# Two-layer graph attention and a typed graph convolution on one core: reordering the preparation and the list writes

## The chip, the core and the metric

The kernel runs on one core of a Trainium2 chip. Five engines work side by side, each through its own instruction queue in a fixed order: TensorE (PE, with its weight loads as PEld), VectorE (DVE), ScalarE (ACT), GpSimd (POOL) and SyncE (SP). SP, ACT and POOL also issue DMAs; the indexed ones (gathers and scatters by a column of row numbers) are all issued by POOL. The metric is the device time of one launch in microseconds.

## What is computed

There are N = 1250 nodes of D = 768 numbers and E = 20000 edges, sorted by destination, each with one of 34 types. Cut to what matters:

```python
h = relu(layernorm(x))
# layer 0: two GATv2 attentions, 8 heads and then 1 head
def gatv2(x, src, dst, Ws, bs, Wd, bd, attn):
    fs, fd = x @ Ws + bs, x @ Wd + bd
    logits = einsum('ehd,hd->eh', leaky_relu(fs[src] + fd[dst], 0.2), attn)
    alpha = softmax of logits over the edges of one dst
    return elu(segment_sum(alpha * fs[src], dst))
h1 = layernorm(gatv2(h, ..., attn1) + h) * ln1_w + ln1_b
x = x + layernorm(gatv2(h1, ..., attno)) * lno_w + lno_b
# layer 1: per (type, dst) the mean of h[src], times W_rel[type]; then a normalised graph sum
h = relu(layernorm(x))
h1 = einsum('rni,rio->no', mean_by_type, W_rel) + h @ W_root + b_rgcn
x = x + normalised neighbour sum of (h1 @ W_gcn) + b_gcn
```

Everything is float32.

## The kernel before

**Nodes and slots.** Nodes are sorted by falling in-degree ("rank order") and cut into NT = 10 tiles of 128. Tile k has `CAPS[k]` slots (33, 22, 20, 18, 17, 16, 15, 14, 13, 11, together 179): slot s of a tile holds the s-th incoming edge of each of its 128 nodes, padded. A slot is one gather of 128 source rows.

**Front** (`fast_front`). It loads the edges and x, normalises x into `hT` (columns) and `h0_d` (rows in DRAM), and finds where each node's edges begin: `got` gathers rows of `dst`, `first` counts. A product with `shift` (L832) gives the next node's start and so the degree. Keys made of degree and node number are spread over all partitions by TensorE (L859, L860), and ten VectorE comparisons (L865) count each node's rank. `rank_d` takes a row of four integers per node (node, first, degree, 0), scattered by rank (L880) and read back in rank order into `rk` (L901). With `first` in rank order, windows of 64 packed edges (type x 2048 + source) are gathered from `win_d` (L912), and five rounds of select-by-bit shift each window to its node's first edge; the result is `f.ell`, from which the source indices `f.srci` come (L931).

The source table `fs_d` (x @ W1s with a column of logit parts per head) is made tile by tile by `sources(j)`: 12 products and two bias products on TensorE, two copies on ScalarE, one write by SP. Tiles 0 and 1 are put ahead of the keys in TensorE's order, tile 2 right behind them, the others follow.

**Pairs** (`pairs`, called at the start of the first attention). For every (type, node) the edges of that type are counted and given a column and lane in a list of pairs. VectorE does nearly all of it; TensorE counts over nodes with 0/1 masks (`mask`, three rounds, L970 to L979), and its results are needed in the second half. The outcome is `place`, the list position of each edge. It goes to DRAM (`place_d`) and comes back. Then the pair list `pair_d` is filled with defaults and the tails of `h2_d` and `h1_d` with zeros (L1354 to L1373).

**Attentions** (`attention`). Per slot: one gather into a ring of 24 buffers `fs` (POOL, L1148), the maximum against the negated destination part (VectorE, L1208), the product with the attention vector and its sum (L1213 and L1214 for 8 heads, L1210 for one). Slots are taken in chunks of up to 20; after a chunk comes its softmax, and then `back`: the rows are scaled and summed on TensorE (L1268, L1258), which frees the ring buffer. While a chunk is in `back`, the next is in front. The destination part of a tile needs its rows gathered, transposed and multiplied by W1d (`negated1`, L1416). After a tile's last chunk `finish1` or `finish2` normalises and makes the next stage's inputs, with several GpSimd DMAs and, in `finish2`, two GpSimd additions.

**List writes.** `list_edges(row, slots)` follows a slot's gather. It adds `slots` to a running count and issues one scatter of an edge slot into `pair_d` (POOL, L1152) for every whole one, 179 in all. `rate` is what each slot adds, `rest` what the last slot adds. Before: 0.9 and 60 in the first attention, 0 and 0 in the second:

```python
            if s >= CHUNK or t.k:
                list_edges(row, rate)
            if t.k == NT - 1 and s == t.S - 1:
                list_edges(row, rest)
```

**After that** come the typed products (`first_half`, `second_half`: gather from `h2_d`, transpose, multiply by W_rel, add into `h1_d`), which read the list through `lists`, and the neighbour sums.

A scheduler in the tile framework sets each engine's order from the program's order and its own estimate of times; `tc.issue_after` puts one instruction behind another.

Of the kernel before, what the change touches and what calls it, by code (L numbers as in the profile page):

```python
# [10 lines left out]
F32 = mybir.dt.float32  # L11
# [7 lines left out]
P = 128  # L19
# [8 lines left out]
PT = 4  # L28
DT = 4
# [597 lines left out]
def fast_front(ctx, tc, f, x, src, dst, edge_type, W1s, b1s, W1d, b1d, attn1, attno, W_rel):  # L627
# [34 lines left out]
    rank_d = dram.tile([NP, 4], I32, name="f_rank_d")  # L662
# [9 lines left out]
    f.ell = keepp.tile([P, NT, S0], I32, name="f_ell")  # L672
# [4 lines left out]
    f.place_d = dram.tile([P, NT * S0], I32, name="f_place_d")  # L677
    f.w1d = const.tile([P, KC, D], F32, name="f_w1d")

    with ExitStack() as front:  # L680
# [110 lines left out]

        quarter = SLOPE / (1.0 - SLOPE)
# [14 lines left out]
        def sources(j):  # L807

            n = min(P, N - j * P)
            ps = ps_m.tile([P, 2, 512], F32, name="ps", tag="ag")  # L810
            for half in range(2):
                for k in range(KC):
                    nc.tensor.matmul(ps[:n, half, :QW], hT[:, k, j * P:j * P + n], w1s[:, k, half], start=(k == 0), stop=False)
                last = nc.tensor.matmul(ps[:n, half, :QW], ones_row[:, :n], bias1[:, half], start=False, stop=True)
            o = work.tile([P, H, HD + 1], F32, name="o_s", tag="o_s", bufs=3)
            ov = o.rearrange("p (a h) d -> p a h d", a=2)
            nc.scalar.copy(ov[:n, :, :, :HD], ps[:n, :, :HW].rearrange("p a (h d) -> p a h d", d=HD))
            nc.scalar.copy(ov[:n, :, :, HD], ps[:n, :, HW:QW])
            nc.sync.dma_start(f.fs_d[j * P:j * P + n, :], o[:n].rearrange("p h e -> p (h e)"))
            return last  # L820

        last = sources(0)
# [8 lines left out]
        with tc.issue_after(last.ins):  # L831
            last = nc.tensor.matmul(sh_ps[:, 0:1], shift, first[:, 0:1], start=True, stop=True)  # L832
        with tc.issue_after(last.ins):
            last = sources(1)
# [3 lines left out]


# [14 lines left out]
        with tc.issue_after(last.ins):  # L854
            for g in range(2):
                wide = ps_m.tile([P, 2, 512], F32, name="wide", tag="ag").rearrange("p a b -> p (a b)")
                for lo, hi in ((0, 512), (512, N // 2)):
                    at = slice(g * (N // 2) + lo, g * (N // 2) + hi)
                    nc.tensor.matmul(wide[:, lo:hi], ones16[:EP], flat2[:, at], start=True, stop=False)  # L859
                    last = nc.tensor.matmul(wide[:, lo:hi], big16[:EP], flat[:, at], start=False, stop=True)  # L860
                nc.scalar.copy(keys[:, g * (N // 2):(g + 1) * (N // 2)], wide[:, :N // 2])
# [7 lines left out]
        rec = prep.tile([P, NT, 4], I32, name="rec")  # L869
        nc.vector.memset(rec, 0)  # L870
        nc.vector.tensor_copy(rec[:, :, 0], node)
        nc.vector.tensor_copy(rec[:, :, 1], first[:, :NT])
        nc.vector.tensor_copy(rec[:, :, 2], deg)

        past = prep.tile([NP - N, 4], I32, name="past")
# [10 lines left out]
        with tc.issue_after(last_keys.ins):  # L886
            sources(2)


        packed = prep.tile([EP, EC], I32, name="packed")  # L890
        nc.vector.scalar_tensor_tensor(packed, ev[:, 2, :], 2048.0, ev[:, 0, :], op0=ALU.mult, op1=ALU.add)
        zrow = prep.tile([1, RW], I32, name="zrow")
        nc.vector.memset(zrow, 0)
        pk = packed.rearrange("p (r c) -> p r c", c=RW)
        nc.scalar.dma_start(win_d[1:NR + 1, :RW].rearrange("(p r) c -> p r c", p=EP), pk)
        nc.scalar.dma_start(win_d[0:NR, RW:].rearrange("(p r) c -> p r c", p=EP), pk)
        nc.scalar.dma_start(win_d[NR:NR + 1, RW:], zrow)


        rk = prep.tile([P, NT, 4], I32, name="rk")  # L900
# [3 lines left out]
        nc.vector.tensor_copy(f.degf, rk[:, :, 2])  # L904
        arow = prep.tile([P, NT], I32, name="arow")
        nc.vector.tensor_scalar(arow, rk[:, :, 1], 5, None, op0=ALU.arith_shift_right)
        nc.vector.tensor_scalar(arow, arow, float(NR - 1), 1.0, op0=ALU.min, op1=ALU.add)
        offs = prep.tile([P, NT], I32, name="offs")
        nc.vector.tensor_scalar(offs, rk[:, :, 1], RW - 1, None, op0=ALU.bitwise_and)
        win = prep.tile([P, NT, WIN], I32, name="win")  # L910
        for k in range(NT):
            nc.gpsimd.indirect_dma_start(  # L912
                out=win[:, k, :], out_offset=None, in_=win_d[:, :],
                in_offset=bass.IndirectOffsetOnAxis(ap=arow[:, k:k + 1], axis=0))
        wf = prep.tile([P, NT, WIN], F32, name="wf")
        nc.vector.tensor_copy(wf, win)
        bits = prep.tile([P, 5, NT], F32, name="bits")
        for i in range(5):
            bi = prep.tile([P, NT], I32, name="bi", tag="bi", bufs=2)
            nc.vector.tensor_scalar(bi, offs, i, 1, op0=ALU.arith_shift_right, op1=ALU.bitwise_and)  # L920
            nc.vector.tensor_copy(bits[:, i, :], bi)
        for i in (4, 3, 2, 1, 0):
            b = 1 << i
            L = S0 + b - 1
            df = prep.tile([P, NT, S0 + 15], F32, name="df", tag="df")
            nc.vector.tensor_sub(df[:, :, :L], wf[:, :, b:b + L], wf[:, :, :L])
            nc.vector.tensor_tensor(df[:, :, :L], df[:, :, :L],
                                    bits[:, i, :, None].to_broadcast([P, NT, L]), op=ALU.mult)
            nc.vector.tensor_add(wf[:, :, :L], wf[:, :, :L], df[:, :, :L])
        nc.vector.tensor_copy(f.ell, wf[:, :, :S0])  # L930
        nc.vector.tensor_scalar(f.srci, f.ell, 2047, None, op0=ALU.bitwise_and)  # L931
# [5 lines left out]
        def pairs():  # L937
# [13 lines left out]
            typ = pp.tile([P, NT, S0], I32, name="typ")  # L951
            nc.vector.tensor_scalar(typ, f.ell, 11, None, op0=ALU.arith_shift_right)
            tv = pp.tile([P, NT, S0], F16, name="tv")
            nc.vector.scalar_tensor_tensor(tv, pad, 100.0, typ, op0=ALU.mult, op1=ALU.add)
# [11 lines left out]
            for i in range(3):  # L966
# [11 lines left out]
                for k in range(NT):  # L978
                    nc.tensor.matmul(tp[:, :R], ones_b, mask[:, i, k, :], start=(k == 0), stop=(k == NT - 1))  # L979
# [3 lines left out]
                tot.append(b)  # L983

# [71 lines left out]
            pl_i = pp.tile([P, NT, S0], I32, name="pl_i")  # L1056
# [11 lines left out]
            nc.vector.scalar_tensor_tensor(pl_i, pad, float(P * COLS), pl, op0=ALU.mult, op1=ALU.add)  # L1068
            nc.sync.dma_start(f.place_d[:, :], pl_i.rearrange("p k s -> p (k s)"))

        for j in range(3, NT):
            sources(j)
        rows_only.close()
# [52 lines left out]
def fast_rest(ctx, tc, f, x, src, dst, edge_type, W1s, b1s, W1d, b1d, attn1, ln1_w, ln1_b,  # L1126
# [9 lines left out]
    h2_d = dram.tile([NP + P, D], F32, name="r_h2_d")  # L1136
    ZERO = NP + (PT + 1) * P
    h1_d = dram.tile([ZERO + 1, D], F32, name="r_h1_d")
# [33 lines left out]
    def attention(H, table, negated, attn_e, first, loads, finish, rate, rest):  # L1172
# [21 lines left out]
        def front(c, i):  # L1194
# [5 lines left out]
            if s >= CHUNK or t.k:  # L1200
                list_edges(row, rate)
# [526 lines left out]
```

## Time and profile before

| | us |
|---|---|
| time, median of 3 runs | 2796.56 (2795.64 to 2802.76) |
| the profiled execution, its own time | 2795.48 |
| its span, first to last instruction | 2793.7 |
| mean granted TensorE clock | 0.925 |

| stage | from, to (us) | DVE busy | POOL busy | PE busy |
|---|---|---|---|---|
| front, to the ranks' columns | 45 to 128 | 34.07 | 22.04 | 80.07 |
| pairs and first slots | 128 to 221 | 83.12 | 28.42 | 47.12 |
| first attention, steady | 258 to 813 | 487.90 | 432.28 | 434.67 |
| passage to the second | 813 to 908 | 62.73 | 51.92 | 79.01 |
| second attention, first half | 908 to 1131 | 208.66 | 154.66 | 141.87 |
| second attention, second half | 1131 to 1331 | 194.75 | 145.15 | 176.94 |
| typed products | 1407 to 2590 | 293.73 | 553.99 | 1172.29 |
| sums | 2590 to 2793 | 93.06 | 117.46 | 143.38 |

All rows are of one profiled execution; busy time is in us of the stretch. A line of the timeline gives start and duration in us, the engine, the line of the kernel, the operation, out<-in with sizes, the count, and in brackets how long the engine had been idle and what ended that. A line of the waits gives the total, the number of times and the longest, in us. A stall costs time only where nothing later absorbs it.

### The profile page before, as it was taken

The numbers are of one execution on the slowest core, as the hardware profiler recorded it, in microseconds if no ns is written. First come the engines' busy times: TensorE is split into PE (matmuls) and PEld (weight loads), VectorE is DVE, ScalarE is ACT, GpSimd is POOL, SyncE is SP. The second block draws the span as 40 slices with busy tenths as digits, with TensorE's granted clock in tenths as the row PEclk, the third lists the DMA queues.
The fourth block names the chain that finished last, engine by engine and source line by source line (L and its number), as shares of the span: only waits on it lengthen the run. The fifth ranks groups of instructions, "written<-read, shape, count | busy, mean of one in ns | idle before, by whom it ended". The sixth has DMA issues, their size and how long they took to land. (4 is left out here: it accounts for less than half of the span.)

```text
span 2793.7 us, 23960 instructions
## 1 busy us (share of the span) xinstructions
PE 2345.4 (84%) x7635; PEld 1354.2 (48%) x7635; DVE 1556.5 (56%) x2363; ACT 851.2 (30%) x2295; POOL 1546.9 (55%) x1131
## 2 busy tenths in 40 slices
PE   5953693788988377898789999999999999999667
PEld 3521252444444244454456666666666666665234
DVE  6589969898985899999453222222222222200263
ACT  3003774776772122333311211221221122121000
POOL 1343877777774766776275444444444544431574
PEclk9976896999999789999889999999999999999888
DMA  6144443454531766765387777777777777765785
GB/s 214 45 159 164 131 129 94 120 142 129 143 102 35 267 208 193 220 208 182 123 264 191 190 191 190 186 195 198 197 188 185 194 192 182 182 158 147 235 275 182
DMA packets 137988, 483.91 MB, mean 173 GB/s; under 512 B 26474, under 2 KB 28803, under 8 KB 137854
## 3 DMA queue, kind: packets, MB, share of 16 engines
q0 software_dynamic: 85152, 341.52, 47.1%
q1 hardware_dynamic: 48043, 134.21, 13.6%
q10 hardware_dynamic: 4658, 6.57, 0.7%
q8 instruction: 63, 1.03, 0.1%
q14 instruction: 72, 0.58, 0.1%
HBM read 392.99 MB, written 89.33 MB: 173 GB/s over the span
## 5 line engine op out<-in xcount | busy, mean ns | idle before, releaser
L1116 PE MATMUL ps<-wrel,mT 128*128 128x384 f32 x3336 | 1099.6, 486 | 1.3 <-DMA wrel<-in_L_gnn_W_rel_dram 1.3
L1116 PEld LDWEIGHTS ps<-wrel,mT 128*128 128x128 f32 x3336 | 623.4, 190 | 407.5 <-issue 1.6
L1148 POOL DMA_INDIRECT g<-r_h_d,lists x241 | 340.8, 1414 | 527.6 <-DVE g L1580 282.8
L1268 PE MATMUL ag<-fs,identf 128*128 128x384 f32 x716 | 291.1, 541 | 178.0 <-ACT fs L1266 167.8
L1580 DVE TENSOR_TENSOR g<-g,g 128x768 f32<-128x768 f32 x68 | 64.6, 950 | 620.4 <-DMA g<-r_h_d,lists 304.0
L1208 DVE TENSOR_TENSOR z<-fs,nfd 128x776 f32<-128x776 f32 (+1 forms) x358 | 347.4, 988 | 45.3 <-DMA fs<-f_fs_d,rec 24.9
L1266 ACT ACTIVATE fs<-fs,lg 128x96 f32<-128x96 f32 x1376 | 371.1, 362 | 4.6 <-issue 4.1
L1258 PE MATMUL ag<-fs,dg 128*128 128x384 f32 x716 | 252.4, 514 | 80.6 <-ACT dg L1256 80.0
L1148 POOL DMA_INDIRECT fs<-f_fs_d,rec x179 | 245.0, 1369 | 104.6 <-issue 48.1
L1152 POOL DMA_INDIRECT r_pair_d<-rec,place x179 | 245.8, 1373 | 95.0 <-issue 47.9
L1268 PEld LDWEIGHTS ag<-fs,identf 128*128 128x128 f32 x716 | 136.4, 205 | 321.1 <-ACT fs L1266 244.4
L1603 POOL DMA_INDIRECT r_h_d<-y,lists x139 | 221.8, 1596 | 109.3 <-ACT y L1602 52.9
L1148 POOL DMA_INDIRECT fs<-r_fs_d,rec x179 | 234.9, 1312 | 83.2 <-issue 33.1
L1258 PEld LDWEIGHTS ag<-fs,dg 128*128 128x128 f32 x716 | 142.1, 201 | 187.6 <-ACT dg L1256 85.7
L1602 ACT ACTIVATE y<-ps,lists 128x768 f32<-128x768 f32 x71 | 64.1, 902 | 479.8 <-PE ps L1116 473.0
L1602 ACT ACTIVATE y<-ps,rcnt 128x768 f32<-128x768 f32 x68 | 61.4, 902 | 456.3 <-PE ps L1116 456.3
L1659 DVE TENSOR_TENSOR acc<-acc,nb 128x768 f32<-128x768 f32 x86 | 82.4, 958 | 198.1 <-DMA nb<-r_h_d,srcz 194.2
L1210 DVE SCALAR_TENSOR_TENSOR z<-z,attn_o 128x769 f32<-128x769 f32 x179 | 178.4, 1015 | 0.0
L1213 DVE TENSOR_TENSOR z<-z,attn 128x776 f32<-128x776 f32 x179 | 168.8, 958 | 0.1
L1214 DVE TENSOR_REDUCE lg<-z 128x8 f32<-128x776 f32 x179 | 168.4, 953 | 0.1
L1513 DVE SCALAR_TENSOR_TENSOR arow<-node,from_f,arow 128x1250 f16<-128x1250 f16 x93 | 140.3, 1508 | 1.0
L1104 PEld LDWEIGHTS pt<-identf,g 128*128 128x128 f32 x834 | 100.5, 142 | 55.2 <-issue 24.1
(284 smaller groups left out, 2301.8 us busy)
## 6 DMA issues: line engine op xcount, KB each, us to landing
wrel<-in_L_gnn_W_rel_dram SPq DMA_DIRECT2D x37, 2304.0 KB
g<-r_h_d,lists POOLq DMA_INDIRECT x241
r_nfd_d<-fd SPq DMA_DIRECT2D x10, 384.0 KB
nfd<-r_nfd_d SPq DMA_DIRECT2D x10, 384.0 KB
r_x_d<-xb SPq DMA_DIRECT2D x10, 384.0 KB
x1r<-r_x_d SPq DMA_DIRECT2D x10, 384.0 KB
f_fs_d<-o_s SPq DMA_DIRECT2D x9, 388.0 KB
x<-in_x_dram SPq DMA_DIRECT2D x9, 384.0 KB
```

Source lines behind the costliest of these rows:

```text
L1116: last = nc.tensor.matmul(ps[:n, half, :f.HW], hT[:, k, j * P:j * P + n], w[:, k, cols], start=(k == 0), stop=(k == f.KC - 1 and not bias))
L1148: return nc.gpsimd.indirect_dma_start(out=to, out_offset=None, in_=table, in_offset=bass.IndirectOffsetOnAxis(ap=idx, axis=0))
L1152: s = nc.gpsimd.indirect_dma_start(out=table, out_offset=bass.IndirectOffsetOnAxis(ap=idx, axis=0), in_=rows, in_offset=None, **kw)
L1208: nc.vector.tensor_tensor(z, fs, t.nfd, op=ALU.max)
L1210: nc.vector.scalar_tensor_tensor(z[:, 0, :], z[:, 0, :], 1.0, attn_e[:, 0, :], op0=ALU.mult, op1=ALU.mult, accum_out=t.lg[:, s, :])
L1213: nc.vector.tensor_mul(z, z, attn_e)
L1214: nc.vector.tensor_reduce(t.lg[:, s, :], z, axis=AX.X, op=ALU.add)
L1258: nc.tensor.matmul(c.ps[:, half, :HW], dg, fs[:, 0, half * HW:(half + 1) * HW], start=begin, stop=end)
L1266: nc.scalar.activation(fs[:, h, :HD], fs[:, h, :HD], AF.Copy, scale=t.lg[:, s, h:h + 1])
L1268: nc.tensor.matmul(c.ps[:, half, :HW].rearrange("p (h d) -> p h d", d=HD), f.identf, fs[:, half * H // 2:(half + 1) * H // 2, :HD], start= ...
L1513: nc.vector.scalar_tensor_tensor(a, node16, from_f[:, k, s:s + 1], a, op0=ALU.is_equal, op1=ALU.add)
L1603: s = nc.gpsimd.indirect_dma_start(out=h1_d[:, :], out_offset=bass.IndirectOffsetOnAxis(ap=j.node, axis=0), in_=y, in_offset=None, compute ...
```

## The change

Five things are moved or resized; the arithmetic is the same.

1. `sources(0)` and `sources(1)` no longer stand ahead of the keys; `sources(0)` now follows them, and the others come after the pairs are declared.
2. Windows of edges are gathered by node number, from `first` directly, and shifted to the first edge there. The rows scattered by rank grow from 4 to 2 + 33 integers (node, degree, the packed edges). The second gather after the read-back is gone; `f.srci` and the new `f.typ` come straight from `rk`.
3. The TensorE products of `sources(7)` to `sources(9)` (`TL = 7`) are put behind the pairs' last mask product.
4. The fills of `pair_d`, `h2_d` and `h1_d` move into the front, and `place` stays in SBUF.
5. List writes start with sixteen after slot 23 of the first tile of either attention; rates become 0.7 with 0 at the end, and 0.5 with 60 at the end in the second attention.

```diff
+TL = 7
...
-    rank_d = dram.tile([NP, 4], I32, name="f_rank_d")
+    rank_d = dram.tile([NP, 2 + S0], I32, name="f_rank_d")
...
-    f.place_d = dram.tile([P, NT * S0], I32, name="f_place_d")
+    f.place = keepp.tile([P, NT, S0], I32, name="place")
...
+        fill = prep.tile([P, COLS, 3], I32, name="fill")
+        nc.vector.memset(fill[:, :, 2], 0)
...
+        nc.sync.dma_start(f.pair_d.rearrange("(p c) f -> p c f", p=P), fill)
+        zero = prep.tile([P, D], F32, name="zero")
+        nc.vector.memset(zero, 0.0)
+        nc.sync.dma_start(f.h2_d[NP:, :], zero)
+        for t in range(PT + 1):
+            nc.sync.dma_start(f.h1_d[NP + t * P:NP + (t + 1) * P, :], zero)
...
         def sources(j):
...
+            mine = []
...
-            return last
-
-        last = sources(0)
+            return mine
...
-        with tc.issue_after(last.ins):
-            last = nc.tensor.matmul(sh_ps[:, 0:1], shift, first[:, 0:1], start=True, stop=True)
-        with tc.issue_after(last.ins):
-            last = sources(1)
+        nc.tensor.matmul(sh_ps[:, 0:1], shift, first[:, 0:1], start=True, stop=True)
...
+        nc.vector.tensor_copy(begin, first[:, :NT])
+        nc.vector.tensor_scalar(arow, begin, 5, None, op0=ALU.arith_shift_right)
...
+        for j in range(NT):
+            nc.gpsimd.indirect_dma_start(
+                out=win[:EP, j, :], out_offset=None, in_=win_d[:, :],
+                in_offset=bass.IndirectOffsetOnAxis(ap=arow[:EP, j:j + 1], axis=0))
...
+        rec = prep.tile([P, NT, 2 + S0], I32, name="rec")
         nc.vector.tensor_copy(rec[:, :, 0], node)
-        nc.vector.tensor_copy(rec[:, :, 1], first[:, :NT])
-        nc.vector.tensor_copy(rec[:, :, 2], deg)
+        nc.vector.tensor_copy(rec[:, :, 1], deg)
+        nc.vector.tensor_copy(rec[:EP, :, 2:], wf[:EP, :, :S0])
...
         with tc.issue_after(last_keys.ins):
-            sources(2)
+            sources(0)
...
+        nc.vector.tensor_scalar(f.srci, rk[:, :, 2:], 2047, None, op0=ALU.bitwise_and)
+        nc.vector.tensor_scalar(f.typ, rk[:, :, 2:], 11, None, op0=ALU.arith_shift_right)
...
                 for k in range(NT):
-                    nc.tensor.matmul(tp[:, :R], ones_b, mask[:, i, k, :], start=(k == 0), stop=(k == NT - 1))
+                    ahead = nc.tensor.matmul(tp[:, :R], ones_b, mask[:, i, k, :], start=(k == 0), stop=(k == NT - 1))
...
+            for i in behind:
+                tc.add_manual_dep(i.ins, ahead.ins.name, mybir.DependencyInfo(
+                    mybir.DependencyClass.NoSync, mybir.DependencyReason.DATA), reason="the table's last tiles later")
...
-            nc.vector.scalar_tensor_tensor(pl_i, pad, float(P * COLS), pl, op0=ALU.mult, op1=ALU.add)
-            nc.sync.dma_start(f.place_d[:, :], pl_i.rearrange("p k s -> p (k s)"))
-
-        for j in range(3, NT):
+            nc.vector.scalar_tensor_tensor(f.place, pad, float(P * COLS), pl, op0=ALU.mult, op1=ALU.add)
+
+        for j in range(1, TL):
             sources(j)
+        behind = []
+        for j in range(TL, NT):
+            behind += sources(j)
...
-            if s >= CHUNK or t.k:
+            if t.k == 0 and s == ring - 1:
+                list_edges(row, 16)
+            elif t.k or s >= ring:
                 list_edges(row, rate)
...
-        attention(H, f.fs_d, negated1, f.attn_1, prepare_lists, loads1, finish1, 0.9, 60)
+        attention(H, f.fs_d, negated1, f.attn_1, prepare_lists, loads1, finish1, 0.7, 0)
...
-        attention(1, fs2_d, negated2, f.attn_o, lambda: None, loads2, finish2, 0, 0)
+        attention(1, fs2_d, negated2, f.attn_o, lambda: None, loads2, finish2, 0.5, 60)
```

## The prediction

> **What bounds the kernel now.** I read the windows by stage first, then who waited for whom inside them, then the timelines where one wait ends another. The kernel is a chain of stages with little overlap between them: front (0 to 221 us), first attention (to about 908), second attention (to about 1390), the typed products, the sums. What a stage saves or loses is passed on whole: the products that follow keep TensorE busy for 1172.29 of 1183 us and are not touched.
>
> The front, VectorE's waits between 45 and 128 us (total, times, longest):
>
> ```profile
> DVE f_perm L902 <- DMA rk<-f_rank_d: 18.8, 1, 18.8
> DVE wf L916 <- issue: 11.9, 1, 11.9
> DVE junk L865 <- ACT keys L861: 10.0, 1, 10.0
> DVE first L835 <- PE sh_ps L832: 5.4, 1, 5.4
> DVE gotf L824 <- DMA got<-in_dst_dram,row_i: 1.9, 1, 1.9
> ```
>
> 48 of 83 us are waits: for TensorE behind two tiles of the source table (L835, L865), for the ranks to go through memory and back (L902), for the edge windows gathered in rank order after that (L916). TensorE meanwhile works on the table to the end, and the pairs' products come behind it:
>
> ```profile
> 66.11 0.39 PE L859 MATMUL wide<-diag,ones 125*128 125x512 f16 x1
> ...
> 141.95 4.15 PE L813 MATMUL ps<-w1s,hT 128*98 128x388 f32 x12
> 146.03 0.89 PE L814 MATMUL ps<-bias,ones_row 1*98 1x388 f32 x2
> 146.85 0.32 PE L970 MATMUL pp<-mask,tri 128*128 128x340 bf16 x1
> ```
>
> Both attentions, busy us per engine (PE, PEld, DVE, ACT, POOL, each with its count):
>
> ```profile
> 258.00:813.00 555.00, 434.67 (x1251) 228.90 (x1249) 487.90 (x671) 382.23 (x1329) 432.28 (x307) 0.90 0.46 127
> 908.00:1131.00 223.00, 141.87 (x404) 79.89 (x403) 208.66 (x398) 51.08 (x113) 154.66 (x115) 0.82 0.70 220
> ```
>
> VectorE leads in both (88% and 94%), but a GpSimd DMA row is followed by 0.30 us of issue, so GpSimd's queue is occupied for 432.28 + 307 x 0.3 = 524 of 555 us, and for about 189 of 223. How near the second attention is to the limit is in its GpSimd timeline:
>
> ```profile
> 944.70 1.45 POOL L1148 DMA_INDIRECT fs<-r_fs_d,rec  x1 [0.30 <-issue]
> 946.45 1.53 POOL L1148 DMA_INDIRECT xt<-in_x_dram,f_permg  x1 [0.30 <-DVE lg L1223]
> 951.69 1.81 POOL L1467 TENSOR_TENSOR xt<-xt,lnb 128x768 f32<-128x768 f32 x1 [3.71 <-DMA xt<-in_x_dram,f_permg]
> 953.64 1.51 POOL L1148 DMA_INDIRECT fs<-r_fs_d,rec  x1
> ...
> 962.44 1.45 POOL L1148 DMA_INDIRECT fs<-r_fs_d,rec  x1 [0.30 <-DVE z L1208]
> 964.19 1.44 POOL L1148 DMA_INDIRECT fs<-r_fs_d,rec  x1 [0.30 <-DVE z L1210]
> 965.94 1.45 POOL L1148 DMA_INDIRECT fs<-r_fs_d,rec  x1 [0.30 <-DVE z L1208]
> ```
>
> From 955 to 980 the gathers start exactly 1.75 us apart. That is VectorE's time for a slot there (L1208 and L1210, 0.875 us from start to start each): GpSimd gets one DMA through per slot. With VectorE idle (front, 104 to 116 us) the same kind of row takes 0.95, so 1.25 with its issue. There is nearly no room for a second one per slot.
>
> **The change, part by part.** All sums are made against the profiled execution: 2795.48 us, span 2793.7. The median of the three runs, 2796.56, is 1.1 above it.
>
> (1) Sources(0) and (1) leave TensorE's queue ahead of the keys. `first` stands at 50.9; the shift product (0.4 us) now meets an idle TensorE, so L835 waits 0.6 instead of 5.4. Then 2.1 us of degrees and diagonals, to 53.7, and the keys' products with their copies, 2.45 us (66.11 to 68.56 in the trace), to 56.2: wait 2.6 instead of 10.0. Saved 12.2 us. Ranking, 10 x 1.56, ends at 72.
>
> (2) Windows in node order. Four small DVE operations of 0.1 us, ten gathers on GpSimd (0.95 + 0.30 in the trace; 1.5 + 0.3 allowed beside ranking) from 52.5 to 65 or 71, landing 2.9 us later by the attention's shortest gather-to-use time. Either is about covered by ranking: the wait of 11.9 goes. If the cover fails, 2 us come back. The 9.4 us of selection (118.15 to 127.55) stay, ahead of the scatter now, which starts at 82.5 instead of 84.7. Rows grow from 16 to 140 bytes, no more of them; ten scatters at 1.18 + 0.30 and 3.85 us to the landed read-back as now, plus at most 3 for longer rows: ranks and edges are in at 101.6. Behind the scatter on GpSimd nothing stands until the first attention; behind the read-back on SP stand the table's writes, as today (100.66 in the trace), and three `o_s` buffers carry those until about 105. The pairs start at 103.3 instead of 128.3: 25.0 saved.
>
> (3) The table. Sources(0) starts after the keys, at 55.5; a tile takes 9.91 us (57 to 147 in the trace), so seven end at 124.9. The pairs' masks, 18 us after the pairs' start as now, are there at 121.3. The products take 6.8 (146.85 to 153.6), to 131.7; the last three tiles end at 161.4, 14.6 later than now. On VectorE the part that needs no products (16 us) lasts until 137.5, so the products are hidden; the remaining pair work (26 us of the old 162 to 190 stretch and 14.6 us of picks now woven between slots) ends near 179. The rows gathered at 162, transposed and multiplied by W1d (10.4 us) are ready at 180. So VectorE waits 1 to 2 us. If the scheduler leaves picks behind that wait, up to 15 are lost: upper end.
>
> (4) The fill. 2.6 us of DVE (223.5 to 226) and eight SP writes of 2.7 MB move ahead of ranking, into time when SP has issued its loads (idle from 18.4 to 27.3) and DVE waits (4 us before 23.3); h0's writes, not read before 150, go behind them. Saved 2.6; the gather of `got` may land 1 us later. `place` stays in SBUF; its trip through DRAM was hidden.
>
> Front: -25.0 - 2.6 + 1.5 + 1 = **-25**, between -30 and -5.
>
> (5) List writes in the first attention. Sixteen go after gather 23, in the gap before the ring of 24 buffers frees (187 to 258 in the trace, four writes in it): free. Then 0.7 per slot for 155 slots: 124 in all, 55 are left. The 36 of the old remainder lie behind the last gather beside work of TensorE and VectorE (the row write they hold up is ready at 842.7, issued at 873.9, but the next user of its buffer waits for TensorE until 878.5): no gain. In the steady part about 30 writes less stand against 24.9 us, in 20 waits, in which VectorE stood for gathered rows. After such a wait it often meets the next one, for TensorE or ScalarE, so I take a third: **-9**, between -2 and -25.
>
> (6) List writes in the second attention: none before, now 16 after gather 23 and 39 over the next 78 slots. Behind gather 23 are the gathers of slot 24 on; the first of them is used 6.1 us after its issue ends (961.2), 3 of which are landing. Of the sixteen, nine go at 1.75 until VectorE runs dry at 961, seven at 1.25: 24 us later for gather 24, 3 of slack: 21 lost. Then 39 x 1.5 (between both prices) = 58 more on GpSimd. Its queue stood free between 950 and 1131 for 26 us, less the 0.3s (ring 7.5, L1089 9.2, root 5.0, den 4.2): 32 lost. Sum **+53**. Low end: 1.25 each, all gaps used, the other DMAs 0.2 faster: +18. High end: 1.75 each, nothing used: +93. I stay by the rows nearest to it. After slot 101 all is as before; VectorE can't make up for it.
>
> Here a rule speaks against the price. The Trainium skill, "SBUF — State Buffer", section "Who interferes with whom", reports a probe in which tensor_tensor and tensor_reduce did not stall DMAs that GpSimd issues, as they leave free the write interface that descriptors need. By it a write beside L1208 and L1210 costs 1.25 and the sum is -25 - 9 + 18, about -16. The rows above (1.45 at a full VectorE, 0.95 at an idle one) contradict it for these indexed DMAs, and decide.
>
> Sum: -25 - 9 + 53 = **+19**: 2814.5, and 2815 on the median's scale.
>
> **Rivals.** *The writes fit (faster).* GpSimd speeds up as VectorE pauses, the gaps take the rest, part 6 costs 10 instead of 53, part 5 gives 15: -25 - 15 + 10 = -30, 2767. For it: 34 of 223 us of the queue are free. Against: 16 writes in a row behind gather 23, and 1.75 per gather right after. It decides below a cost of about 34 for part 6. *Even.* Part 6 at 35: within a few us of now, about 2797. *The front also fails (slower).* ScalarE's dinv, which today waits 14.9 us for the degrees inside the table's copies, or SP's read of the ranks, falls one tile earlier in the order; TensorE stalls 7 us, picks stay behind the late nfd: the front saves 5 only, +39, 2835. *Not as said.* If the three tiles still ran ahead of the products, VectorE would wait from 137 to 162: front 0, 2841.
>
> **How the numbers follow.** Forecast 0.50 (2800 to 2840 alone), front fails 0.16, even 0.14, fit 0.20. About 0.3% (8 us) is what this kernel's measurement tells from no change. Faster 0.20, same 0.14, slower 0.66. Range 2780 to 2850: it leaves out the deep end of "fit" and the high end of part 6.
>
> **What would show it.** Right: keys' wait under 3 us, `win` landed before selection, pairs from 103, table end near 161, place near 180, the second attention's first z about 34 us earlier (near 879); then z waits for fs rows of 50 us instead of 19, and a second attention some 50 longer. Wrong: those waits below 30, or first z later than 895.

## The result, and the profile after

The changed kernel takes 2863.86 us (median of 4 runs) against 2799.37 for the kernel before (median of 4): ratio 1.023, 95% interval 1.0205 to 1.0255. It is 64 us slower. The forecast was 2815, with a range of 2780 to 2850. The sign was right; the time lies outside the range.

The two profiled executions (2863.54 and 2795.48 us) are read against each other at marks that both have. "First max" is the first L1236 (L1208 before) of an attention, "18th" and "21st" are that operation of the 18th and the 21st slot of the first attention; the slots end with the last such operation of an attention.

| mark (us) | before | after | difference |
|---|---|---|---|
| ranks and edges read, pairs start | 128.3 | 113.3 | -15.0 |
| table's last product | 146.1 | 180.2 | +34.1 |
| `place` made | 220.6 | 183.0 | -37.6 |
| first max | 191.7 | 206.7 | +15.0 |
| 18th slot | 251.7 | 251.9 | +0.2 |
| 21st slot | 258.4 | 273.8 | +15.4 |
| end of the first attention's slots | 844.5 | 847.0 | +2.5 |
| second attention, first max | 912.6 | 916.0 | +3.4 |
| second attention, end of its slots | 1329.9 | 1393.2 | +63.3 |
| last typed product | 2581.4 | 2642.3 | +60.9 |
| last instruction | 2793.7 | 2861.8 | +68.1 |

The column reads as four steps. The front gives nothing by the 18th slot (forecast: 25 gained). The first attention loses 15 between its 18th and 21st slot and regains 13. The second attention loses 60 (forecast: 53). The last stage, behind the typed products, takes 7 more. The second attention's first z, for which the prediction named "later than 895" as a sign of being wrong, came at 916.0.

Every mark is of one execution. In another one of the unchanged kernel after (`e14_after_again` below) the first attention's slots end at 838.6 instead of 847.0, so differences of a few us between single marks mean little.

VectorE's waits between 45 and 128 us, kernel after (total, times, longest):

```profile
DVE f_perm L954 <- DMA rk<-f_rank_d: 19.3, 1, 19.3
DVE wf L918 <- issue: 6.7, 1, 6.7
DVE gotf L853 <- DMA got<-in_dst_dram,row_i: 3.8, 1, 3.8
DVE junk L913 <- ACT keys L909: 2.2, 1, 2.2
```

The waits for TensorE ahead of the keys went as forecast. A wait for the edge windows is still there, 6.7 of the old 11.9. VectorE's timeline says why: the cast of the windows (L918) stands after the fourth of ten comparisons (L913), and the other six stand behind it.

```profile
66.60 1.51 DVE L913 TENSOR_SCALAR_CACHE_REDUCE junk<-keys,key 128x1250 bf16<-128x1250 f32 x1
68.04 0.08 DVE L913 DVE_READ_ACCUMULATOR junk<-keys,key 128x1 f32 x1
74.80 0.49 DVE L918 CAST wf<-win 125x640 f32<-125x640 int32 x1 [6.68 <-issue]
75.21 1.51 DVE L913 TENSOR_SCALAR_CACHE_REDUCE junk<-keys,key 128x1250 bf16<-128x1250 f32 x1
```

TensorE and ScalarE, kernel after: ScalarE's square root (L1382) waits 29 us for the degrees with the table's copies behind it, so TensorE stands for 11.2 us in the middle of the table.

```profile
101.01 0.91 PE L843 MATMUL ps<-bias,ones_row 1*128 1x388 f32 x2
113.15 5.17 PE L841 MATMUL ps<-w1s,hT 128*128 128x388 f32 x8 [11.23 <-ACT o_s L848]
...
180.13 0.89 PE L843 MATMUL ps<-bias,ones_row 1*98 1x388 f32 x2
```

```profile
112.04 0.30 ACT L1382 ACTIVATE dinv<-f_degf,f_ones_col 128x10 f32<-128x10 f32 x1 [29.01 <-DVE f_degf L956]
```

Behind the table's end comes the chain that VectorE now stands for, 20.5 us, with the picks long done (timeline of all engines, kernel after): gather, transposes, product, `nfd`.

```profile
185.74 0.99 POOL L1174 DMA_INDIRECT h<-f_h_d,f_permg  x1 [78.46 <-DVE nfd L1215]
194.15 1.51 PE L1133 MATMUL pt<-identf,h 128*128 128x128 f32 x6 [13.02 <-DMA bias_s<-in_L_gnn_bos_dram]
195.63 10.02 PE L1145 MATMUL ps<-f_w1d,hT 128*128 128x384 f32 x24
205.69 0.96 DVE L1421 SCALAR_TENSOR_TENSOR nfd<-ps,bias 128x768 f32<-128x768 f32 x1 [20.47 <-PE ps L1145]
```

The burst in the first attention, kernel after (timelines of POOL, ACT and DVE): the next tile's rows are gathered behind the sixteen writes, ScalarE copies their transposes ahead of the first softmax's exponent, and VectorE waits 14.3 us for that exponent.

```profile
261.05 0.97 POOL L1178 DMA_INDIRECT r_pair_d<-rec,place  x1 [0.31 <-issue]
262.33 1.00 POOL L1174 DMA_INDIRECT h<-f_h_d,f_permg  x1 [0.30 <-issue]
...
267.27 1.06 ACT L1135 COPY hT<-pt 128x384 f32<-128x384 f32 x2 [71.10 <-PE pt L1133]
269.65 0.31 ACT L1260 ACTIVATE lg<-lg 128x128 f32<-128x128 f32 x1
269.99 0.38 DVE L1262 TENSOR_REDUCE den<-lg 128x8 f32<-128x128 f32 x1 [14.33 <-ACT lg L1260]
```

The burst in the second attention, kernel after, GpSimd's timeline and then VectorE's:

```profile
962.20 1.45 POOL L1178 DMA_INDIRECT r_pair_d<-rec,place  x1 [0.30 <-issue]
963.95 0.97 POOL L1178 DMA_INDIRECT r_pair_d<-rec,place  x1 [0.30 <-issue]
...
972.89 0.97 POOL L1178 DMA_INDIRECT r_pair_d<-rec,place  x1 [0.30 <-issue]
974.17 0.99 POOL L1174 DMA_INDIRECT xt<-in_x_dram,f_permg  x1 [0.31 <-issue]
978.11 1.80 POOL L1472 TENSOR_TENSOR xt<-xt,lnb 128x768 f32<-128x768 f32 x1 [2.95 <-DMA xt<-in_x_dram,f_permg]
980.06 0.99 POOL L1174 DMA_INDIRECT fs<-r_fs_d,rec  x1
```

```profile
984.09 0.96 DVE L1236 TENSOR_TENSOR z<-fs,nfd 128x769 f32<-128x769 f32 x1 [21.29 <-DMA fs<-r_fs_d,rec]
```

VectorE runs dry at 963, and stands 21.3 us. All its waits for gathered rows in the second attention (19.1 us in 8 before):

```profile
DVE z L1236 <- DMA fs<-r_fs_d,rec: 78.8, 38, 21.3
```

### The profile page after: what moved, and what is told of

It reads as the page before. It is cut to its first block, busy times and chain, and to the rows that moved or that the text cites. A ratio compares the mean times of both kernels' runs of the same rounds, so it can differ in the third digit from the quotient of the medians.

```text
span 2861.8 us, 23950 instructions
## 1 busy us (share of the span) xinstructions
PE 2347.5 (82%) x7635; PEld 1360.0 (48%) x7635; DVE 1553.2 (54%) x2362; ACT 849.6 (30%) x2295; POOL 1555.7 (54%) x1131
## 5 line engine op out<-in xcount | busy, mean ns | idle before, releaser
L1236 DVE TENSOR_TENSOR z<-fs,nfd 128x776 f32<-128x776 f32 (+1 forms) x358 | 340.5, 964 | 99.9 <-DMA fs<-r_fs_d,rec 78.8
L1296 PE MATMUL ag<-fs,identf 128*128 128x384 f32 x716 | 284.6, 532 | 106.4 <-ACT fs L1294 95.1
L1174 POOL DMA_INDIRECT fs<-f_fs_d,rec x179 | 239.1, 1336 | 124.1 <-issue 55.0
L1178 POOL DMA_INDIRECT r_pair_d<-rec,place x179 | 264.9, 1480 | 56.4 <-issue 45.7
L1607 ACT ACTIVATE y<-ps,rcnt 128x768 f32<-128x768 f32 x68 | 61.4, 902 | 456.8 <-PE ps L1145 456.8
L1174 POOL DMA_INDIRECT nb<-r_h_d,srcz x86 | 102.0, 1186 | 47.9 <-DMA nb<-r_h_d,srcz 27.5
```

The lines of the kernel that those rows point to most:

```text
L1174: return nc.gpsimd.indirect_dma_start(out=to, out_offset=None, in_=table, in_offset=bass.IndirectOffsetOnAxis(ap=idx, axis=0))
L1178: s = nc.gpsimd.indirect_dma_start(out=table, out_offset=bass.IndirectOffsetOnAxis(ap=idx, axis=0), in_=rows, in_offset=None, **kw)
L1236: nc.vector.tensor_tensor(z, fs, t.nfd, op=ALU.max)
L1296: nc.tensor.matmul(c.ps[:, half, :HW].rearrange("p (h d) -> p h d", d=HD), f.identf, fs[:, half * H // 2:(half + 1) * H // 2, :HD], start= ...
```

## The experiments

They ran on several chips, on which the kernel before took 2777 to 2795 us (medians); times are therefore given as ratios to the kernel before on the same chip, with their 95% intervals, and marks and waits are of one profiled execution each. On one of these chips the kernel after stood at 1.0238 (1.0203 to 1.0273).

**The lists apart from the front.** `e1_lists_before` is the kernel after with the old condition and rates:

```diff
-            if t.k == 0 and s == ring - 1:
-                list_edges(row, 16)
-            elif t.k or s >= ring:
+            if s >= CHUNK or t.k:
                 list_edges(row, rate)
...
-        attention(H, f.fs_d, negated1, ..., 0.7, 0)
+        attention(H, f.fs_d, negated1, ..., 0.9, 60)
...
-        attention(1, fs2_d, negated2, ..., 0.5, 60)
+        attention(1, fs2_d, negated2, ..., 0, 0)
```

> The changed front with the list writes as in the kernel before (0.9 a slot over the first attention from slot 16 on, the rest at its end, none over the second, no burst of sixteen). Theory L (the loss is the 55 list writes over the second attention): the second attention goes from 477 us (first max to last, kernel after) back to 417, the first attention, which gets 51 writes more, grows from 640 to about 652; time 2864 - 60 + 12 = about 2816. Rival A (a list write costs the same wherever it stands, the front is what lost): the two attentions together stay within 10 us of the kernel after, time 2854 or more.

`e2_lists_only` is the reverse: the kernel before with only these lines changed.

> The kernel before with only the changed rates of list writes (16 behind the 24th gather of each attention, 0.7 a slot, then 0.5 a slot in the second). Theory L: second attention 477 instead of 417 with one wait of about 21 us at the burst, first attention about 10 shorter at most; time 2799 + 60 - 10 = about 2849; what is left between that and the 2864 of the kernel after, 15 us, is then the changed front's. Rival A: within 10 us of 2799, the front bears the whole of the loss.

e1: 1.0017 (0.9997 to 1.0037), second attention 415.5 us. e2: 1.0153 (1.0127 to 1.0179), second attention 477.1. The waits of VectorE there, e1 and then e2:

```profile
DVE z L1234 <- DMA fs<-r_fs_d,rec: 19.2, 11, 8.2
```

```profile
DVE z L1210 <- DMA fs<-r_fs_d,rec: 79.5, 42, 21.3
```

The second attention's 60 us belong to the list writes, whatever the front. Rival A fell, and e1 says that the new front alone gives nothing measurable. e1's first attention did not grow to 652 as I wrote, but took 632.7; it lacks the burst's 15 us. (In the code the single writes of before start at slot 20, `CHUNK`, and not at 16 as this and later expectations say.)

The two ratios add up to 1.017, not 1.024, some 20 us less. Two things are in the marks. In the old front the burst does not disturb the first attention (18th to 21st slot 6.7 us; 21.9 in the kernel after). And in e2 the old front itself was faster than in the profile of before: its 18th slot came at 242.3 instead of 251.7, with VectorE's operations in the same order. Between 160 and 193 us VectorE pauses for 8.4 us in before (8.8 in e8 below, which has the old front too), none of them put down to another engine or a DMA, and for 0.4 in e2, a wait for TensorE. The same operation, before and then e2:

```profile
175.86 0.51 DVE L1011 TENSOR_TENSOR pdf<-pdf,xcol 128x340 f32<-128x340 f32 x1 [1.79 <-issue]
```

```profile
169.97 0.51 DVE L1011 TENSOR_TENSOR pdf<-pdf,xcol 128x340 f32<-128x340 f32 x1
```

No kernel with the new front has such pauses there. What makes them was not tried. So how much a front gains depends on the execution it is held against: by e2's 18th slot the new front loses 9.6 us instead of 0.2.

**Bursts.** `e9_no_second_burst` and `e12_no_first_burst` take one burst each out of the kernel after (`if H > 1 and t.k == 0 ...`, `if H == 1 and t.k == 0 ...`).

> The kernel after without the burst of sixteen in the second attention: all of its 55 writes come at 0.5 a slot. If the burst's wait (21.3 us) is a cost of its own, the second attention falls from 477 to about 456 and the time by 0.7%. If GpSimd is the bound there and each write costs its own time wherever it stands, the wait of 21.3 us goes and the same time comes back as more and smaller waits for gathers: second attention 470 or more, time within 7 us of the kernel after.

> The kernel after without the burst of sixteen in the first attention; the second attention gets its burst and, with 16 more writes left over, 0.5 a slot for longer. If the burst costs the first attention what the slots show (from the 18th to the 21st slot 21.9 us instead of 7.5): the 21st slot's max at about 259 instead of 273.8 and the first attention's end 12 to 15 us earlier, then 16 writes more over the second attention at about 1.1 us each, 17 us: the time within 6 us of the kernel after. If the first attention is bound by VectorE over its length and the burst's stall is taken up: its end within 4 us of 847, and the time 15 us longer than the kernel after's.

e9: 1.0221 (1.0187 to 1.0255), second attention 469.5 instead of 477.2 (in an execution 15 us faster than e9's median). The wait of 21.3 is gone and most of its time is back as small waits:

```profile
DVE z L1236 <- DMA fs<-r_fs_d,rec: 69.9, 48, 9.4
```

So most of what a write costs there is its own time on GpSimd, wherever it stands; the burst adds 8 us at most, and the two kernels' ratios do not tell them apart. That it is GpSimd's queue and not the traffic of the DMAs fits the second attention's windows: with 0.30 us for each of its operations GpSimd is occupied for about 448 of 477 us in the kernel after (362 of 418 before), while the DMA engines' busy share falls from 0.69 to 0.62. e12: 1.0245 (1.0226 to 1.0263); 18th to 21st slot 7.5 us as expected, and the 16 writes more make the second attention 491.7. What the first attention gains between those slots (14.4) the second loses (14.5): the total stays where it was.

`e16_first_burst_only` puts the first burst into the mended kernel described below, with all writes over the first attention.

> The mended front with all list writes over the first attention (0.9 a slot, the rest at its end), and with the burst of sixteen behind its 24th gather in place of the single writes of slots 16 to 23: as many writes as in the mended kernel, only bunched. If the burst costs what the slots of the kernel after show: the 21st slot's max 15 us later than in the mended kernel, and of that 10 us or more still there at the first attention's end; time about 12 us longer. If the first attention takes the stall up later: the same 15 at the 21st slot, less than 4 at the end, same time.

18th to 21st slot 24.7 us instead of 7.5, time 1.0011 (0.9985 to 1.0037) against the mended kernel's 0.9986 on the same chip: medians 2795.35 and 2783.50, 12 us. In the two profiled executions the first attentions end within 1 us of each other; but the mended one's execution was itself 8.7 us above its median, so I go by the medians, and where the 12 us are carried stays unshown. Nor is it the bunching alone: with single writes from slot 20 on, the sixteen replace about four writes, so that twelve more fall into the first attention and twelve fewer behind its last gather.

**Writes in the passage.** `e8_before_slow_lists` is the kernel before with 0.7 a slot from slot 24 and the rest at the first attention's end.

> The kernel before with its list writes at 0.7 a slot from slot 24 on instead of 0.9 from slot 16 on, no burst, and all that are left (about 70) at the end of the first attention, none over the second. Theory L': the 24 us that the first attention's end gained with the changed rates in the front of before came from fewer writes beside it, and the second attention's loss is apart from it: first attention's end at about 822, of the 70 writes (about 100 us of GpSimd at 1.45) some 20 to 40 us stick out past the passage between the attentions, so the second attention's first max is near 905 and the time within 10 us of before. Rival: the burst or the order that goes with it made that gain: first attention's end at 840 or later, time 2815 or more.

1.0071 (1.0047 to 1.0095): slower by more than expected. The first attention's slots end at 824.5 instead of 844.5, so theory L' was right that fewer writes there save time (20 us for 34 writes, 0.6 each); but 54 writes in the passage push the last row of `fs2_d` from 61.4 to 99.1 us behind that (37.7 for 34 more, 1.1 each). The second attention's price in the kernel after is 60 / 55 = 1.1 each. Of the three places the first attention is the cheapest in these executions, and that is where most of them had been.

**The front's waits.** `e3_dinv_late` and `e5_win_after` take away one wait each:

```diff
+        with tc.issue_after(f.last_table):
             nc.scalar.activation(f.dinv, f.degf, AF.Sqrt, ...)
...
+        with tc.issue_after(ranked.ins):
             nc.vector.tensor_copy(wf[:EP], win[:EP])
```

> The kernel after with one instruction of ScalarE, the square root of the degrees, put behind the table's last copy; the read of the ranks stays on the SyncE queue between the table's writes. Theory F (that instruction holds ScalarE and so TensorE): the stall of 11.2 us at 101.9 goes or shrinks to under 3, since ScalarE still has one free buffer of three when the writes stand behind the read; the table ends near 170 instead of 181, the first max falls at about 196 instead of 207, and if the front's end sets the first attention's the time is about 2854. Rival S (the read on SyncE is as bad as the instruction): stall 8 or more, table end 178 to 181, time 2861 to 2864. Rival R (the first attention takes up a late start): first max 10 earlier, its end unmoved, time 2862.

> The kernel after with the cast of the gathered windows put behind the last comparison of the ranking (in the kernel after it stands behind four of ten and waits 6.7 us for the windows). Theory F: the wait goes, the rank scatter starts at 86 instead of 92.7, the pairs at 106.6 instead of 113.3, TensorE's stall behind ScalarE falls from 11.2 to about 4.5, the table ends at 174, first max at about 200, time 2857. Rival R: the same marks earlier but the first attention's end unmoved, time 2863.

`e6_front_fix` has both, and the read of the ranks on GpSimd's queue (`nc.gpsimd.dma_start(rk, ...)`); `e7_front_fix_lists_before`, "the mended kernel", has the old list writes as well.

> The kernel after with three orders changed in the front: ScalarE's square root behind the table, the windows' cast behind the ranking, and the read of the ranks on the GpSimd queue, which has nothing else there, so that no write of the table stands behind it. The list writes are as in the kernel after. Theory F (what the front lost is these waits): no stall of TensorE in the table, table from 60 to about 160 with the products between, pairs from 106, first max at about 183 to 186 instead of 207, first attention's end about 22 earlier than in the kernel after, time about 2.0% less than the kernel after's less what the burst takes, ratio to before about 1.015. Rival P (one of the two waits hides the other, so each of them alone gives what both give): first max at 190 or later, ratio 1.019.

> The same three orders and the list writes as in the kernel before. If the front's gain, forecast at 25 us, is there once its waits are gone: first max 183, first attention about 633 long as in the run with the list writes of before, its end about 816, time about 25 us under that run, ratio to before about 0.993. If the first attention takes up an earlier start (bound by the gathers or the picks): its end within 8 us of 841, ratio 1.000 or more.

| | after | e3 | e5 | e6 | e7 |
|---|---|---|---|---|---|
| table's last product | 180.2 | 165.5 | 168.8 | 165.5 | 167.0 |
| first max | 206.7 | 195.2 | 190.7 | 190.4 | 188.9 |
| 18th slot | 251.9 | 240.4 | 235.8 | 235.6 | 234.1 |
| 21st slot | 273.8 | 257.4 | 264.2 | 260.2 | 241.6 |
| ratio | 1.023 | 1.0195 | 1.0199 | 1.0164 | 0.9954 |

In each of e3, e5 and e6 TensorE's stall is gone. Theory F holds for the marks. Its rival P holds for the cast: e5 alone moves the 18th slot by 16.0 us, e6 by 16.2. The square root alone (e3) moves it by 11.5. In e5 the square root still waits 13.3 us, but at a place in the order where TensorE has buffers left: no wait of TensorE in that table is over 0.6. The burst takes part of it back (18th to 21st slot 28.4 us in e5). e7 has no burst: its interval is 0.994 to 0.9969, faster than the kernel before on that chip. The front's gain, once its waits are out, is 17.6 us at the 18th slot (251.7 to 234.1), not 25; held against e2's execution of the old front (242.3) it is 8.2.

`e11_products_behind` is e7 with `TL = 10`, the products behind the whole table.

> The same mended front with the pairs' products behind the table's last tile again, as in the kernel before, and the list writes of before: only the place of the products differs from the fastest run so far. If having the picks done before the first max is what their place buys: the table ends at 160 instead of 167, the picks stand between the first maxima again (first five slots 24 us instead of 11.4), the 18th slot's max at 245 to 250 instead of 234.1, time 10 us or more longer, ratio 0.999 or more. If the picks only fill VectorE's wait for nfd: the 18th slot within 3 us of 234, ratio 0.995.

1.0015 (1.0004 to 1.0026), 18th slot at 243.0. It does not answer its question: the square root was tied to the table's last copy, and in this order VectorE's reciprocal stands ahead of the pair work and waits 19.0 us for it. What the products' place is worth by itself stays open.

**The wait for `nfd`.** In e7 VectorE still stood 12.2 us for the first tile's destination part. `e10_h0_early` gathers its rows into memory of the pairs' pool ahead of the table's end:

```diff
         f.pairs()
+        h0a = f.pp.tile([P, D], F32, name="h0a")
+        gather(h0a, f.h0_d[:, :], f.permg[:, 0:1])
+        hTa = f.pp.tile([P, KC, P], F32, name="hTa")
+        to_columns(nc, ps_t, f, hTa, 0, h0a, P, both=True)
+        f.ps0 = dense(nc, ps_t, f, hTa, f.w1d, 0, P, tag="mm2")
         f.front.close()
```

> The front with its three orders mended and the list writes of before (the fastest so far), and the first tile's destination rows gathered and transposed ahead of the table's end, into memory of their own (a second gather fetches them again for the residual), so that only their product with the weights, 9.4 us, comes behind the table. The step of the forecast that this tests: VectorE was to wait 1 to 2 us for nfd, and waits 12.2 in that run and 20.5 in the kernel after. If the gather's place behind the table's end makes that wait: nfd at about 178 instead of 188, VectorE waits under 4, first max near 179, and if the first attention carries it through, its end 10 us earlier, ratio to before about 0.992. If the gathers of the first slots or the loads of the two weights that start at 175 bound the first slots: first max earlier, the 18th slot's no more than 3 us earlier, ratio as before that change, 0.995.

Neither outcome: 0.9986 (0.9977 to 0.9995) on a chip where e7 did not run, rows gathered at 107.6, but the first max still at 188.9. TensorE's timeline names what took over: the second half of the transposes waits for `none`, VectorE's last read of the pairs' flag, whose product lies in the bank of PSUM (tag `ptc0`) that the transposes share.

```profile
169.29 0.18 PE L1091 MATMUL fl_ps<-badc,ones_b 128*128 128x1 bf16 x1
175.48 0.90 PE L1135 MATMUL pt<-identf,h0a 128*128 128x128 f32 x3 [6.01 <-DVE none L1093]
176.95 10.96 PE L1147 MATMUL ps<-f_w1d,hTa 128*128 128x384 f32 x24 [0.57 <-ACT hTa L1137]
```

`e13_flag_own_bank` is e10 with the flag in a bank that the table has left:

```diff
-            fl_ps = ps_t.tile([P, 512], F32, name="fl_ps", tag="ptc0")
+            fl_ps = ps_m.tile([P, 2, 512], F32, name="fl_ps", tag="ag")[:, 0, :]
```

> The run with the first tile's rows gathered and transposed early, and the picks' flag put into a bank of PSUM that the table has left instead of the one that the transposes use. If the bank was what still held the product with the weights (it waited for the flag's last read at 175.3): the product stands right behind the table's last tile, 169 to 179, nfd at about 180, VectorE's wait for it 2 to 4 us instead of 10 to 12, first max at about 181 instead of 189, the 18th slot's at 226 instead of 234, and the time 8 us under that of the mended kernel on the same chip. If the gathered rows bound the first slots instead: first max 181, 18th slot 231 or later, time within 3 us of the mended kernel's.

It ran with `e15_mended_again` (e7 unchanged) and `e14_after_again` (the kernel after unchanged) on one chip.

> The mended front with the list writes of before, unchanged, beside the three others on one chip: about 2.7% under the kernel after (0.9954 against 1.023 in two different chips), ratio to before 0.994 to 0.999; first max 189, 18th slot 234.

> The kernel after, unchanged, beside the three others on one chip: ratio to before about 1.023; marks of the front as in its own profile (pairs 113, first max 207, 18th slot 252, 21st 274).

TensorE and VectorE of e13:

```profile
167.56 0.18 PE L1091 MATMUL fl_ps<-badc,ones_b 128*128 128x1 bf16 x1
167.60 7.99 PE L1147 MATMUL ps<-f_w1d,hTa 128*128 128x384 f32 x24
...
178.39 0.96 DVE L1430 SCALAR_TENSOR_TENSOR nfd<-ps,bias 128x768 f32<-128x768 f32 x1
```

`nfd` no longer waits at all. First max 179.4 (192.5 in e15), 18th slot 225.4 (237.6), 21st 239.6 (245.1): of 12 us more than half is lost again, since VectorE now reaches the exponent earlier than ScalarE does, and waits 6.7 us there. Time 0.9968 (0.995 to 0.9986) against e15's 0.9986 (0.9974 to 0.9998): medians 2778.20 and 2783.50, with intervals that overlap a little. The kernel after took 2857.36 there, so e13 is 2.8% under it. The mended kernel itself stands at 0.9986 here and stood at 0.9954 on e7's chip, and these two intervals do not touch: differences of 0.3% between chips say nothing about a change.

`e17_lists_from_24` starts the list writes of e13 at slot 24, 0.95 a slot.

> The fastest run so far (first tile's rows early, the flag in its own bank), with the single list writes from slot 24 on at 0.95 instead of from slot 16 on at 0.9, about 30 left for the passage; the gathers of the next tile's rows then stand ahead of every write. If the chain of gather, ScalarE's copy and the exponent behind it is what holds VectorE there: its wait of 6.7 us for the exponent is under 1.5, the 21st slot's max comes 7.5 us after the 18th's instead of 14.2, the first attention's end 5 us earlier less what the ten more writes in the passage take, ratio to before 0.995 to 0.997. If GpSimd's own time bound these slots: 12 us or more from the 18th to the 21st, ratio 0.998 or more.

0.9979 (0.9968 to 0.999). The wait stayed, and no write stands ahead of it any more (VectorE's waits, then the timelines of GpSimd and ScalarE):

```profile
DVE den L1262 <- ACT lg L1260: 6.8, 1, 6.8
```

```profile
222.91 3.76 POOL L1176 DMA_INDIRECT h<-f_h_d,f_permg  x1 [0.30 <-issue]
226.97 0.95 POOL L1176 DMA_INDIRECT h<-f_h_d,f_permg  x1 [0.30 <-issue]
...
230.79 1.08 ACT L1137 COPY hT<-pt 128x384 f32<-128x384 f32 x2 [64.75 <-PE pt L1135]
```

The expectation missed because the gather stands behind the ring's 24 gathers too. The chain gather, copy, exponent is what VectorE waits for by the timelines; in the kernel after the sixteen writes lengthen it. No run moved that gather ahead.

## Why the prediction was wrong, point by point

The total, +19, was the sum of -25, -9 and +53. Measured at the marks: about 0 (18th slot), +2.3 (from there to the first attention's end) and +60. **The step that failed is (3), its last link: "ready at 180. So VectorE waits 1 to 2 us".** `nfd`'s product was ready at 205.7 instead of 180: the table ended 19.6 later, the gather behind it went 4.2 later, and the chain took 2 longer. VectorE waited 20.5, and with that the front's -25 was gone.

- *(1) Keys no longer behind the table.* The waits came out as forecast (2.2 for the keys instead of 2.6, the shift product's gone). But ranking started at 61.9, not 56.2: `first` stood at 55.9, not 50.9. VectorE's work ahead of it ended 3.3 us later with the fill in it, and `got` kept it waiting 1.9 longer. Step (4) had charged 1 us for this; it was 5.
- *(2) Windows covered by ranking.* The cover was there, and the order did not use it: the cast went into the middle of the ranking. I had costed that wait at nothing, with at most 2 us if the cover failed; it was 6.7, and e5 removes it. Pairs started at 113.3, not 103.3: ranking began 5.7 later and the cast cost 6.7; the selection behind it took 2 less than charged.
- *(3) The table.* Table end 181, not 161: 5.8 from the later start, 11.2 from ScalarE's square root, and 2.3 in the twelve products right behind that stall, which took 6.47 us instead of 4.18. That was the rival *the front also fails*, word for word (dinv one tile earlier, a stall of 7), at a chance of 0.16. Then I let the first tile's gather go at 162, 0.6 us behind the table, though in the profile of before it went 4.8 us behind it (146.85 to 151.61); in the kernel after it went 4.8 behind again. The chain from gather to `nfd` took 20 us (forecast 18). `place`, forecast at 179, was there at 183, though the pairs started 10 us late. That it came so near was luck: the forecast had counted 6.8 us of VectorE's pauses in the old stretch from 162 to 190 as work, and the kernel after does not have them. With the picks done, nothing was left to do beside the chain. In the kernel before, the same wait had been filled with picks. First max against first max was the wrong yardstick: before, 15 us of picks lay between the first 18 maxima (60.0 us for them, 45.2 after), so the front's balance must be read at a slot behind them. e13 shows that this chain can be hidden.
- *(5) First attention, -9.* The lower rate gave 13 us from the 21st slot on, more than forecast (20 in e14, and 20 in e8 without a burst). "Sixteen go after gather 23 ... free" was wrong: 15.4 us, through ScalarE's queue. I had asked whether GpSimd had time, and not which gather stands behind the writes and who reads it.
- *(6) Second attention, +53.* Right in mechanism and nearly in size: 21 lost at the burst (measured 21.3), then 32 (39). The waits for rows grew from 19.1 to 78.8; "about 50" was too low. e9 adds that the burst's 21 us are for the most part no cost of its own: without it the stage still takes 469.5.
- *The rule that was weighed* would have made the total -16. The rows decided for the dearer price, and rightly: 1.45 while VectorE works, 0.97 as soon as it is dry.
- *Not forecast:* the last stage took 219.5 us instead of 212.3, with the same code. It took 212 to 220 in the other runs, and neither the front nor the lists divide these; its cause was not tried.

With the rival of the front taken for the main case the sum had been +39. The first attention at +2.3 instead of -9 and the second at +60 instead of +53 make it +57; the front, which gave nothing instead of 5, and the last stage's 7 are the rest of the 68.

## What to carry to other kernels

Cost a moved or lengthened piece of work by what stands behind it on each engine's fixed order, not only by whether its own engine has time: here one square root, one cast and one gather, each a microsecond or less of work, cost 11, 7 and 14 us. When work that filled a wait is pulled ahead, look for the wait that it filled. And a stage whose queue has hardly a free place for each slot pays nearly the full price for every further transfer, bunched or spread.

## What the hardware showed

In the first attention a GpSimd transfer with an index column does not slow down beside VectorE's operations with two inputs in SBUF, it waits for their end. Timeline of VectorE and GpSimd in the first attention's burst, kernel after:

```profile
227.72 1.83 DVE L1236 TENSOR_TENSOR z<-fs,nfd 128x776 f32<-128x776 f32 x2
228.50 3.67 POOL L1178 DMA_INDIRECT r_pair_d<-rec,place  x1 [0.30 <-issue]
229.47 1.83 DVE L1241 TENSOR_TENSOR z<-z,attn 128x776 f32<-128x776 f32 x2
231.22 1.81 DVE L1242 TENSOR_REDUCE lg<-z 128x8 f32<-128x776 f32 x2
232.48 0.97 POOL L1178 DMA_INDIRECT r_pair_d<-rec,place  x1 [0.30 <-issue]
```

The row that starts at 228.50 ends at 232.17, 0.95 us after the first reduction begins: it stood through the maxima and the products, which have two inputs in SBUF, and then took as long as the row behind it, 0.97. The rows that start at 233.75, 238.98 and 244.22 end 0.92 to 0.93 us after a first reduction begins. So two transfers pass for each pair of slots here, both beside the reductions, and none between one two-input operation and the next. In the second attention, where the maximum and the product with its sum both have two inputs, one passes per slot in 1.45 us; what lets it through there these rows do not show.

The Trainium skill, "SBUF — State Buffer", section "Who interferes with whom", from which the prediction took its remark on a probe, also states that a VectorE instruction with two SBUF inputs contends with a GpSimd instruction that reads SBUF. The rows above agree with that sentence, and not with the remark that tensor_tensor did not stall transfers that GpSimd issues.
